# Eight of thirty bases of a graph layer summed by TensorE in column groups, and loads moved to another queue

## The chip, the cores and the metric

The kernel runs on one core of a Trainium2 chip, as one launch. The metric is the device time in microseconds of that launch; the profile describes one execution of it, and its span goes from the first to the last instruction of the trace.

## The reference

The input is a graph of N = 625 nodes with H = 512 features and E = 10000 edges of two relations. All is float32. Three blocks are computed:

```python
xn = layernorm(x)
# graph block: two layers; row, col = src, dst
w = einsum('rb,bio->rio', att, basis)        # 30 bases of 512x512 -> 2 relation matrices
msg_r = sigmoid(xn[col] @ gate_w[r])[:, None] * xn[col] @ w[r]     # by the edge's relation
h = relu(segment_sum(msg, row) + xn @ root1 + bias1)
out = the same with h, basis2, att2, gate_w2, root2, bias2
# mix block: linear attention with random features over xn, then a dense pair
x = x + out + mix(xn)
# feed-forward block: a shared expert, and two banks of 8 experts with top-1 routing
x = x + ffn(layernorm(x))
```

What matters here is `w`: for each layer, 30 bases of 1 MB are read from memory and summed into two matrices (r = 0, 1), each base with a coefficient `att[r, b]`.

## The kernel before

There is a fast path (`tile_fast`) and a general one, which runs only if a flag says that the edges are not sorted as expected; in these runs the fast path gives the result. All lines below are of the fast path.

The nodes stand in NT = 5 tiles of 125 (TP); the features in KC = 4 blocks of 128. A matrix of 512x512 is held as 128 partitions x 4 x 512.

**The stream of bases.** `relation_weights(l)` (L798) builds `wrel[l]`, 128 x 2 x 4 x 512, for layer l. For each of the 30 bases it issues a load of 1 MB on SP's queue (L806) into one of three slots of the tile `bases`, and then two operations, one per relation: the first base is scaled by ScalarE (L811), each later base is multiplied by its coefficient and added by VectorE (L813, scalar_tensor_tensor over 2048 elements in each of 128 partitions). A slot is loaded again when its two operations are done. Both layers' streams are written out early, with a low priority (`tc.cur_priority` raised by 100000): a scheduler at build time puts each instruction into its engine's program by priority and by the times that it expects, and on the chip each engine then goes through its own program in that order.

**The order on each engine.** On VectorE, operations of the stream stand between the operations of the rest of the kernel. On TensorE the order is: the mix block, with the counting of edges between it (L932, one-hot matrices that give `cnt`, how many edges lead from node to node by relation); then layer 1, `gathered` (L1026) and `through` (L1049); then layer 2 in the same way; then the feed-forward block.

`gathered(l, src, gate)` multiplies the features by the gates, as a high part (ScalarE, L1035) and a low rest (VectorE, L1036), and sums over the edges by matmuls with `cnt` (L1044), evacuated by ScalarE (L712). `through(t, ...)` makes one node tile of a layer's output in one PSUM tile by `narrow` (L762, matmuls at L765): a bias row, four matmuls with `root`, eight with `wrel[l]`. Layer 1's output goes through a relu on ScalarE to `gpre` (L1057). Layer 2 needs `gpre` transposed (`flip`, L743; matmuls at L748), its gates (`gates`, L771; ScalarE's exponential at L780, VectorE at L781 and L782), then `gathered`, then `through` (L1139), after which VectorE adds and normalizes.

**Buffers.** Tiles with a tag share memory in turn. In SBUF: "w8" has three buffers, through which wk, wv, wq, wo, w1, w2, root1, root2 and ws go; "A" to "D", "X" and "U" have one each; `yp`, opened after the mix block, has four buffers "y". In PSUM there are `pp` (two tiles of 1024 columns), `pc` (one such tile, tag "cnt") and `pn` (two tiles of 512). After the mix block `wide_ps` (L736) takes every third tile from `pc`.

**Loads other than bases.** They are issued by POOL's queue: wo, w1, w2, the roots (L663), x a second time (`again`, L1060, into the buffer "A" that `xnT` leaves), the shared expert's weights `ws` (L1073), the first weights of both banks (`load_first`, L1093), the second ones of the second bank (L1101). The second weights of the first bank are on SP (L1101, into the buffer that `bases` leaves).

Of the kernel before, what the change touches and what calls it, by code (L numbers as in the profile page):

```python
# [18 lines left out]
N = 625  # L19
H = 512  # L20
# [17 lines left out]
BASES = 3  # L38
MARGIN = 2
STEPS = [range(max(0, EC // NT * m - MARGIN), min(EC, EC // NT * (m + 1) + MARGIN)) for m in range(NT)]  # L40
WIN = 128
NW = (N + NX * (WIN - 1)) // WIN
WHOLE = 1.5 * 2 ** 23
# [544 lines left out]
def tile_fast(ctx: ExitStack, tc: tile.TileContext, a: dict, out: bass.AP, flag):  # L588
# [173 lines left out]
    def narrow(pairs, m=TP, n=H):  # L762
        ps = pn.tile([128, 512], F32, tag="narrow", name="ps_narrow")
        for i, (s, mv) in enumerate(pairs):
            nc.tensor.matmul(ps[:m, :n], s, mv, start=(i == 0), stop=(i == len(pairs) - 1))  # L765
        return ps[:m, :n]

    def nodes(t):
        return slice(t * TP, (t + 1) * TP)
# [14 lines left out]
    def columns(rows, name):  # L784
# [9 lines left out]
    between = {1: lambda: load_w(wkqv[:, 2 * H:3 * H], "wv", nc.sync),  # L794
               2: lambda: load_w(wkqv[:, H:2 * H], "wq", nc.sync)}
    came = {}

    def relation_weights(l):  # L798
        basis = a["L0_gnn_basis1" if l == 0 else "L0_gnn_basis2"]
        w = main.tile([128, 2, KC, H], F32, name=f"wrel{l}")  # L800
        wrel[l] = w
        here = tc.cur_priority
        tc.cur_priority = here + 100000
        for b in range(NB):
            src = bases[:, (l * NB + b) % BASES, :]
            nc.sync.dma_start(src.rearrange("p (k f) -> p k f", k=KC), basis[b].rearrange("(k p) f -> p k f", p=128))  # L806
            for r in range(2):
                dst = w[:, r].rearrange("p k f -> p (k f)")
                s = att_b[l][:, r * NB + b:r * NB + b + 1]
                if b == 0:  # L810
                    nc.scalar.activation(dst, src, AF.Copy, scale=s)  # L811
                else:
                    nc.vector.scalar_tensor_tensor(dst, src, s, dst, op0=ALU.mult, op1=ALU.add)  # L813
            if l == 0 and b in between:
                came[b] = between[b]()
        tc.cur_priority = here

# [21 lines left out]

    relation_weights(0)
    relation_weights(1)
    wv, wq = came[1], came[2]


# [179 lines left out]
    def gathered(l, src, gate):  # L1026
        aggT = main.tile([128, 2, KC, NP], F32, tag="U", name=f"agg{l}")
        for r in range(2):
            for half in range(2):
                hs = slice(half * HF, (half + 1) * HF)  # L1030
                high = yp.tile([TP, NT, HF], F32, tag="y", name=f"high{l}", bufs=4)
                low = yp.tile([TP, NT, HF], F32, tag="y", name=f"low{l}", bufs=4)
                for t in range(NT):
                    s = gate[:, t, r:r + 1]
                    nc.scalar.activation(high[:, t, :].bitcast(F32R), src[:, t, hs], AF.Copy, scale=s)  # L1035
                    nc.vector.scalar_tensor_tensor(low[:, t, :].bitcast(F32R), src[:, t, hs], s, high[:, t, :],  # L1036
                                                   op0=ALU.mult, op1=ALU.subtract)
                for k in range(KC // 2):
                    ks = slice(k * 128, (k + 1) * 128)
                    ps = wide_ps("ps_agg").rearrange("p (s n) -> p s n", s=2)  # L1040
                    pairs = [(y[:, m, ks].bitcast(F32R), m) for y in (high, low) for m in range(NT)]
                    for i, (y, m) in enumerate(pairs):
                        for s in range(2):
                            nc.tensor.matmul(ps[:, s, :SEG], y, cnt[:, r, m, s * SEG:(s + 1) * SEG].bitcast(F32R),  # L1044
                                             start=(i == 0), stop=(i == len(pairs) - 1))
                    evac(aggT[:, r, half * 2 + k, :].rearrange("p (s n) -> p s n", s=2), ps[:, :, :SEG])
        return aggT

    def through(t, srcT, root, aggT, w, more):  # L1049
        return narrow([more] + [(srcT[:, k, nodes(t)], root[:, k, :]) for k in range(KC)]  # L1050
                      + [(aggT[:, r, k, nodes(t)], w[:, r, k, :]) for r in range(2) for k in range(KC)])

    agg1 = gathered(0, xn, gate1)
    gpre = fourth("C", "gpre")
    for t in range(NT):
        ps = through(t, xnT, root1, agg1, wrel[0], (all_rows, brow[:, 1, :]))
        nc.scalar.activation(gpre[:, t, :], ps, AF.Relu)  # L1057

    again = fourth("A", "x_again", (TP + 2, NT, H))
    load_rows(again, a["x"], nc.gpsimd)  # L1060
    for i, nm in enumerate(("L0_mix_b2", "L0_gnn_bias2")):
        s = a[nm]
        nc.gpsimd.dma_start(again[TP + i:TP + i + 1], bass.AP(tensor=s.tensor, offset=s.offset,
                                                             ap=[[0, 1], [0, NT], [1, H]]))
    gT = fourth("B", "gT", TALL)
    flip(gT, gpre)
    gates(gate2, gT, col["gate2"], "ps_gate2")
# [1 line left out]

    ws = main.tile([128, 2, KC * FF], F32, tag="w8", name="ws", bufs=3)
    nc.gpsimd.dma_start(ws[:, 0, :].rearrange("p (k f) -> p k f", f=FF),  # L1073
                        a["L0_ffn_Ws1"].rearrange("(k p) f -> p k f", p=128))
    nc.gpsimd.dma_start(ws[:, 1, :], a["L0_ffn_Ws2"])
    ws1, ws2 = ws[:, 0, :].rearrange("p (k f) -> p k f", f=FF), ws[:, 1, :]

    wr = const.tile([128, KC, 2, NX], F32, name="wr")
    b2x = yp.tile([2 * NX + 1, H], F32, tag="y", name="b2x", bufs=4)
    br_b = const.tile([TP, 2, NX], F32, name="br_b")  # L1080
    for i, nm in enumerate(("sp", "fq")):
        s = a["L0_ffn_br_" + nm]
# [5 lines left out]
    def load_first(nm, tag, more):  # L1088

        t1 = main.tile([128, NX * KC * FF + more], F32, tag=tag, name="we1_" + nm)  # L1090
        s1 = a["L0_ffn_W1_" + nm]
        for e in range(0, NX, 2):
            nc.gpsimd.dma_start(t1[:, e * KC * FF:(e + 2) * KC * FF].rearrange("p (x f) -> p x f", f=FF),  # L1093
                                s1[e:e + 2].rearrange("e (k p) f -> p (e k) f", p=128))
        return t1

    def load_second(nm, tag, more, eng):

        t2 = main.tile([FF, NX * H + more], F32, tag=tag, name="we2_" + nm)
        for e in range(0, NX, 4):  # L1100
            eng.dma_start(t2[:, e * H:(e + 4) * H].rearrange("f (e d) -> f e d", d=H),  # L1101
                          a["L0_ffn_W2_" + nm][e:e + 4].rearrange("e f d -> f e d"))
        return t2

    we1 = [load_first("sp", "wrel0", 0), load_first("fq", "cnt", NW * WIN)]
    we2 = [load_second("sp", "basis", NW * WIN, nc.sync)]


    before = const.tile([TP, TP], F16, name="before")
    nc.gpsimd.memset(before, 1.0)  # L1110
    nc.gpsimd.affine_select(before, before, compare_op=ALU.is_ge, fill=0.0, base=-1, pattern=[[1, TP]],
                            channel_multiplier=-1)
    every = const.tile([TP, 128], F16, name="every")
    nc.gpsimd.memset(every, 1.0)
    lower = const.tile([2 * NX, 2, 2 * NX], F32, name="lower")
    nc.gpsimd.memset(lower, 1.0)
# [38 lines left out]


    G = 2 * NT
    work = yp.tile([128, 2 * NT * HF // 2], F32, tag="y", name="work", bufs=4)
    used = [0]

    def small_tile(*shape):

        n = 1
        for d in shape[1:]:
            n *= d
        used[0] += n
        names = "abcd"[:len(shape) - 1]
        return work[:shape[0], used[0] - n:used[0]].rearrange(
            f"p ({' '.join(names)}) -> p {' '.join(names)}", **dict(zip(names, shape[1:])))
# [221 lines left out]
```

## Time and profile before

| | us |
|---|---|
| median of 3 runs | 554.82 (553.94 to 555.72) |
| the profiled execution | 553.96, span 552.2 |
| PE (TensorE) busy | 454.8, 82% of the span |
| DVE (VectorE) busy | 394.8, 71% |
| of it the stream's 116 operations (L813) | 266.1, mean 2.346 |
| ACT (ScalarE) busy | 187.5, 34% |
| POOL busy | 58.4, 11% |
| chain that ended last | PE 68%, DVE 12%, issue 8%, DMA 7% |
| DMA | 98.29 MB, mean 178 GB/s |

PEld is the weight load of TensorE, which overlaps its matmuls. A float32 matmul appears in the records as two, each with its weight load. "Idle before" with a name after an arrow says how long an engine stood still before an instruction, and what ended the wait. A line number is that of the helper that issues the instruction, so the tiles' names tell groups of one line apart. Busy time is an average over stages: a change is judged by the stage in which it stands.

### The profile page before, as it was taken

What the parts mean: (1) busy time and instruction counts of PE and PEld (TensorE: products, weight loads), DVE (VectorE), ACT (ScalarE), POOL (GpSimd) and SP (SyncE); (2) the same over time, 40 slices, a digit from 0 to 9 for tenths busy, and PEclk for the clock granted to TensorE, in tenths of its full rate; (3) what the DMA queues carried; (4) which work ended last, traced back from release to release, by engine and by line L of the source; (5) the groups of instructions that cost most, each with busy time, mean ns of one, the idle gap of its engine ahead of it and who ended that gap; (6) DMA issues with size and microseconds to landing.
All of it is one profiled execution on the core that took longest, in us unless ns stands there. A gap on an engine that the chain in (4) does not pass through costs nothing.

```text
span 552.2 us, 5413 instructions
## 1 busy us (share of the span) xinstructions
PE 454.8 (82%) x1881; PEld 282.8 (51%) x1881; DVE 394.8 (71%) x477; ACT 187.5 (34%) x304; POOL 58.4 (11%) x105
## 2 busy tenths in 40 slices
PE   1799999999998999999997995009999999966800
PEld 0553486776567547934446992004446556556200
DVE  3789899989898999899997998993221445233311
ACT  2741299979776203500003630000001302321200
POOL 6400000000000000000012011000001080040040
PEclk9999999999897999999997899558999759987955
DMA  8967754633513485767679569634003251440532
GB/s 218 402 233 245 264 179 151 228 98 133 199 61 122 153 286 210 236 216 233 228 239 318 223 203 362 204 146 161 29 19 97 93 144 44 166 132 25 225 105 90
DMA packets 49171, 98.29 MB, mean 178 GB/s; under 512 B 5870, under 2 KB 5994, under 8 KB 49138
## 3 DMA queue, kind: packets, MB, share of 16 engines
q1 hardware_dynamic: 40322, 78.95, 42.0%
q0 software_dynamic: 8816, 18.93, 10.9%
q8 instruction: 17, 0.28, 0.2%
q14 instruction: 16, 0.13, 0.1%
HBM read 89.00 MB, written 8.85 MB: 177 GB/s over the span
## 4 chain that ended last, share of the span: by engine, by line
PE 68%; DVE 12%; issue 8%; DMA 7%; ACT 2%; POOL 1%; DVEq 0%; SPq 0%; POOLq 0%; ACTq 0%
PE ps_narrow L765 39%; PE ps_wide L759 10%; DVE wrel L813 7%; PE ps_agg L1044 5%; PE ps_hid L1329 4%; PE ps_cnt L932 3%; DMA got<-back,slot_i 3%; DMA basis_sb<-in_L_gnn_basis_dram 2%; PE ps_gate L777 2%; PE ps_flip L748 2%; DMA x<-in_x_dram 1%; POOL got L1339 1%; DVE oh_source L929 1%; PE ps_router L1175 1%; PE ps_sT L1320 1%
## 5 line engine op out<-in xcount | busy, mean ns | idle before, releaser
L813 DVE SCALAR_TENSOR_TENSOR wrel<-basis_sb,att,wrel 128x2048 f32<-128x2048 f32 x116 | 266.1, 2346 | 8.6 <-ACT wrel L811 4.4
L765 PE MATMUL ps_narrow<-wrel,agg 128*125 128x512 f32 x160 | 72.2, 606 | 34.2 <-DVE wrel L813 34.2
L927 ACT ACTIVATE side<-iota_h,ed_f 125x630 f16<-125x630 f16 x96 | 71.8, 812 | 7.0 <-PE ps_cnt L932 7.0
L765 PEld LDWEIGHTS ps_narrow<-wrel,agg 128*125 128x125 f32 x160 | 30.7, 193 | 74.3 <-issue 39.1
L932 PEld LDWEIGHTS <-oh_source 125*125 125x125 f16 x192 | 25.9, 139 | 27.2 <-issue 16.9
L932 PE MATMUL ps_cnt<-side,oh_source 125*125 125x315 f16 x192 | 39.0, 305 | 0.2
L1044 PE MATMUL ps_agg<-cnt,high 125*128 125x314 f32 x160 | 29.3, 332 | 5.8 <-ACT high L1035 3.5
L1044 PEld LDWEIGHTS ps_agg<-cnt,high 125*128 125x128 f32 x160 | 26.2, 206 | 6.4 <-ACT high L1035 3.5
L1140 DVE TENSOR_TENSOR v<-v,ps_narrow 125x512 f32<-125x512 f32 x5 | 3.4, 688 | 36.3 <-PE ps_narrow L765 36.3
L725 ACT ACTIVATE ln_rs<-ln_mv,eps 125x1 f32<-125x1 f32 (+1 forms) x7 | 2.1, 299 | 79.8 <-DVE ln_mv L1142 79.8
L929 DVE TENSOR_SCALAR oh_source<-iota_h,col_m,ed_f 125x128 f16<-125x128 f16 x96 | 25.0, 310 | 5.4 <-PE ps_cnt L932 5.4
L1044 PE MATMUL ps_agg<-cnt,low 125*128 125x314 f32 x160 | 27.7, 316 | 0.0
L1342 DVE SCALAR_TENSOR_TENSOR v<-got,work,v 125x512 f32<-125x512 f32 x10 | 7.5, 752 | 24.8 <-DMA got<-back,slot_i 24.8
L1044 PEld LDWEIGHTS ps_agg<-cnt,low 125*128 125x128 f32 x160 | 24.9, 194 | 0.2
L1335 DVE COPY stage<-ps_narrow 128x512 f32<-128x512 f32 x12 | 8.3, 691 | 21.9 <-PE ps_narrow L765 21.9
L1329 PE MATMUL ps_hid<-sort_fq,stage 128*128 x96 | 15.2, 335 | 8.7 <-DVE stage L1326 7.2
L1057 ACT ACTIVATE gpre<-ps_narrow 125x512 f32<-125x512 f32 x5 | 3.0, 597 | 54.6 <-PE ps_narrow L765 54.6
L759 PE MATMUL ps_wide<-zT,wq 128*128 128x512 f32 (+1 forms) x64 | 20.6, 433 | 0.0
L1329 PEld LDWEIGHTS ps_hid<-sort_fq,stage 128*128 128x128 f32 x96 | 14.8, 249 | 9.0 <-issue 7.3
L1339 POOL DMA_INDIRECT got<-back,slot_i x10 | 12.2, 1221 | 66.9 <-DVE sort_fq L1321 32.4
L765 PE MATMUL ps_narrow<-root,xnT 128*125 128x512 f32 x40 | 18.5, 605 | 0.0
L765 PE MATMUL ps_narrow<-wv,zT 128*125 128x512 f32 x40 | 18.4, 603 | 0.0
(271 smaller groups left out, 684.7 us busy)
## 6 DMA issues: line engine op xcount, KB each, us to landing
basis_sb<-in_L_gnn_basis_dram SPq DMA_DIRECT2D x60, 1024.0 KB
back<-stage SPq DMA_DIRECT2D x24, 256.0 KB
w<-in_L_mix_W_dram POOLq DMA_DIRECT2D x2, 1024.0 KB, 5.7
root<-in_L_gnn_root_dram POOLq DMA_DIRECT2D x2, 1024.0 KB
we_sp<-in_L_ffn_W_sp_dram POOLq DMA_DIRECT2D x4, 512.0 KB, 12.3
we_fq<-in_L_ffn_W_fq_dram POOLq DMA_DIRECT2D x4, 512.0 KB, 9.8
we_sp<-in_L_ffn_W_sp_dram SPq DMA_DIRECT2D x2, 1024.0 KB
we_fq<-in_L_ffn_W_fq_dram POOLq DMA_DIRECT2D x2, 1024.0 KB, 5.9
```

Source lines behind the costliest of these rows:

```text
L748: nc.tensor.transpose(ps[:, t, :TP], src[:, t, k * 128:(k + 1) * 128], ident[:TP, :TP])
L759: nc.tensor.matmul(ps[:, lo:hi], s, m[:, lo:hi], start=(i == 0), stop=(i == len(pairs) - 1))
L765: nc.tensor.matmul(ps[:m, :n], s, mv, start=(i == 0), stop=(i == len(pairs) - 1))
L777: nc.tensor.matmul(ps[:TP, 2 * t:2 * t + 2], srcT[:, k, nodes(t)], gw[:, k, :], start=(k == 0), stop=(k == KC - 1))
L813: nc.vector.scalar_tensor_tensor(dst, src, s, dst, op0=ALU.mult, op1=ALU.add)
L927: later(lambda: nc.scalar.activation(side, iota_h[:EP], AF.Sign, bias=row_f[:, c:c + 1]))
L929: later(lambda: nc.vector.tensor_scalar(os, iota_h[:EP, :128], col_m[:, m, c:c + 1], code_f[:, c:c + 1], op0=ALU.is_equal, op1=ALU.mult))
L932: nc.tensor.matmul(ps[:TP, s, :SEG + 1], os[:, :TP], side[:, s * SEG:(s + 1) * SEG + 1], start=(c == STEPS[m][0]), stop=(c == STEPS[m][-1]))
L1044: nc.tensor.matmul(ps[:, s, :SEG], y, cnt[:, r, m, s * SEG:(s + 1) * SEG].bitcast(F32R), start=(i == 0), stop=(i == len(pairs) - 1))
L1329: nc.tensor.matmul(ps, w1s[:, k * FF:(k + 1) * FF], sortT[i][:, k * N:][:, bass.ds(start[w], WIN)], start=(k == 0), stop=(k == KC - 1))
L1335: (nc.vector.tensor_copy if w % 2 else nc.scalar.copy)(y, ps)
L1339: nc.gpsimd.indirect_dma_start(yg[:, t, :], None, back_d[i][:, :], bass.IndirectOffsetOnAxis(ap=slot_i[:, 2 * t + i:2 * t + i + 1], axis=0))
```

## The change

Layer 2's stream is cut to 22 bases. The last eight (QUADS = 2 groups of four) are loaded by POOL into a tile of their own, `quad`, in a buffer of "w8". For each block k of 128 rows and each group q, four loads of 256 KB bring 128 rows of four bases, so that partition 32 j + p holds, for c = 0 to 3, row 32 c + p of base j. A stationary matrix `coef[:, q, r, :]` of 128 x 32 (four identity matrices of 32 x 32, each times its coefficient, made by 16 operations of POOL) then sums the four bases: a matmul for each r and c writes 32 rows, at partitions 32 c, of a PSUM tile of the tag "cnt". After both groups VectorE adds that tile to `wrel[1][:, :, k, :]`.

x is loaded again, and the two biases with it, through SP at priorities that follow the stream's (`stream[0]`), as are the first expert weights of both banks and the second ones of the first bank. In `through` the bias row comes after the root matmuls. `ws`, the routing masks `before` and `every`, and the biases with `mT` (`seconds`) lie in buffers "y" in place of tiles of their own.

```diff
+QUADS = 2
...
+    stream = [None]
     def relation_weights(l):
...
         here = tc.cur_priority
-        tc.cur_priority = here + 100000
-        for b in range(NB):
+        tc.cur_priority = stream[0] or here + 100000
+        for b in range(NB if l == 0 else NB - 4 * QUADS):
...
+        stream[0] = tc.cur_priority
         tc.cur_priority = here
+    def coefficients():
+        coef = const.tile([128, QUADS, 2, 32], F32, name="coef")
+        for q in range(QUADS):
+            for r in range(2):
+                for j in range(4):
+                    p = slice(32 * j, 32 * j + 32)
+                    c = r * NB + NB - 4 * (QUADS - q) + j
+                    nc.gpsimd.tensor_scalar(coef[p, q, r, :], ident[p, 32 * j:32 * j + 32], att_b[1][p, c:c + 1],
+                                            None, op0=ALU.mult)
+        return coef
+
+    def quads(coef):
+        t_ = main.tile([128, KC, H], F32, tag="w8", name="quad", bufs=3)
+        for k in range(KC):
+            ps = pc.tile([128, 2, H], F32, tag="cnt", name="ps_quad")
+            for q in range(QUADS):
+                for j in range(4):
+                    b = NB - 4 * (QUADS - q) + j
+                    nc.gpsimd.dma_start(t_[32 * j:32 * j + 32], a["L0_gnn_basis2"][b, k * 128:(k + 1) * 128, :]
+                                        .rearrange("(c p) f -> p c f", p=32))
+                here = tc.cur_priority
+                tc.cur_priority = here - 3000
+                for r in range(2):
+                    for c in range(4):
+                        nc.tensor.matmul(ps[32 * c:32 * c + 32, r, :], coef[:, q, r, :], t_[:, c, :],
+                                         start=(q == 0), stop=(q == QUADS - 1))
+                tc.cur_priority = here
+            nc.vector.tensor_tensor(wrel[1][:, :, k, :], wrel[1][:, :, k, :], ps, op=ALU.add)
...
     relation_weights(0)
     relation_weights(1)
+    coef = coefficients()
...
     def through(t, srcT, root, aggT, w, more):
-        return narrow([more] + [(srcT[:, k, nodes(t)], root[:, k, :]) for k in range(KC)]
+        return narrow([(srcT[:, k, nodes(t)], root[:, k, :]) for k in range(KC)] + [more]
                       + [(aggT[:, r, k, nodes(t)], w[:, r, k, :]) for r in range(2) for k in range(KC)])
 
     agg1 = gathered(0, xn, gate1)
+    quads(coef)
...
     again = fourth("A", "x_again", (TP + 2, NT, H))
-    load_rows(again, a["x"], nc.gpsimd)
+    here = tc.cur_priority
+    tc.cur_priority = stream[0]
+    load_rows(again, a["x"])
...
-        nc.gpsimd.dma_start(again[TP + i:TP + i + 1], bass.AP(tensor=s.tensor, offset=s.offset,
+        nc.sync.dma_start(again[TP + i:TP + i + 1], bass.AP(tensor=s.tensor, offset=s.offset,
...
+    stream[0] = tc.cur_priority
+    tc.cur_priority = here
...
-    ws = main.tile([128, 2, KC * FF], F32, tag="w8", name="ws", bufs=3)
+    ws = yp.tile([128, 2, KC * FF], F32, tag="y", name="ws", bufs=4)
...
-    b2x = yp.tile([2 * NX + 1, H], F32, tag="y", name="b2x", bufs=4)
+    seconds = yp.tile([2 * NX + 1, H + N], F32, tag="y", name="seconds", bufs=4)
+    b2x = seconds[:, :H]
...
-            nc.gpsimd.dma_start(t1[:, e * KC * FF:(e + 2) * KC * FF].rearrange("p (x f) -> p x f", f=FF),
-                                s1[e:e + 2].rearrange("e (k p) f -> p (e k) f", p=128))
+            nc.sync.dma_start(t1[:, e * KC * FF:(e + 2) * KC * FF].rearrange("p (x f) -> p x f", f=FF),
+                              s1[e:e + 2].rearrange("e (k p) f -> p (e k) f", p=128))
...
+    here = tc.cur_priority
+    tc.cur_priority = stream[0]
     we1 = [load_first("sp", "wrel0", 0), load_first("fq", "cnt", NW * WIN)]
     we2 = [load_second("sp", "basis", NW * WIN, nc.sync)]
-    before = const.tile([TP, TP], F16, name="before")
+    tc.cur_priority = here
...
+    before = small_half(TP, TP)
...
-    every = const.tile([TP, 128], F16, name="every")
+    every = small_half(TP, 128)
...
-    mT = yp.tile([2 * NX + 1, N], F32, tag="y", name="mT", bufs=4)
+    mT = seconds[:, H:]
```

More of the change, by code (lines that the diff above doesn't have):

```diff
@@ L1103, in load_second, with small_tile, small_half @@
         return t2
+    here = tc.cur_priority
+    tc.cur_priority = stream[0]
     we1 = [load_first("sp", "wrel0", 0), load_first("fq", "cnt", NW * WIN)]
     we2 = [load_second("sp", "basis", NW * WIN, nc.sync)]
-    before = const.tile([TP, TP], F16, name="before")
+    tc.cur_priority = here
+    work = yp.tile([128, 2 * NT * HF // 2], F32, tag="y", name="work", bufs=4)
+    used = [0]
+    def small_tile(*shape):
+        n = 1
+        for d in shape[1:]:
+            n *= d
+        used[0] += n
+        names = "abcd"[:len(shape) - 1]
+        return work[:shape[0], used[0] - n:used[0]].rearrange(
+            f"p ({' '.join(names)}) -> p {' '.join(names)}", **dict(zip(names, shape[1:])))
+    def small_half(p, n):
+        used[0] += (n + 1) // 2
+        return work[:p, used[0] - (n + 1) // 2:used[0]].bitcast(F16)[:, :n]
+    before = small_half(TP, TP)
     nc.gpsimd.memset(before, 1.0)
@@ L1157, in tile_fast @@
     G = 2 * NT
[L1158 to L1169, printed above, removed]
     lg = small_tile(TP, G, NX)
```

## The prediction

> **What bounds the kernel now.** I read the waits first, then the order in time of VectorE and of TensorE around the longest wait on the chain that ended last, then windows. In the list of waits (engine and line, what it waited for, total, times, longest) the largest on TensorE is one wait for the second layer's weights:
>
> ```profile
> PE ps_narrow L765 <- DVE wrel L813: 34.2, 1, 34.2
> ```
>
> VectorE in order of time (start, length, line, tiles, count, idle before):
>
> ```profile
> 234.98 63.44 DVE L813 SCALAR_TENSOR_TENSOR wrel<-basis_sb,att,wrel 128x2048 f32<-128x2048 f32 x28 [2.45 <-DMA basis_sb<-in_L_gnn_basis_dram]
> 301.32 0.17 DVE L781 TENSOR_SCALAR gate<-gate 125x10 f32<-125x10 f32 x1 [2.89 <-ACT gate L780]
> ...
> 343.13 31.77 DVE L813 SCALAR_TENSOR_TENSOR wrel<-basis_sb,att,wrel 128x2048 f32<-128x2048 f32 x14 [1.75 <-DMA basis_sb<-in_L_gnn_basis_dram]
> ```
>
> Before 298.4 VectorE has done 30 of layer 2's 58 steps (2.27 us each: 63.44/28). It then breaks off for gate2 and the low halves, so that TensorE can aggregate in the meantime; the last step ends at 372.6. TensorE in order of time:
>
> ```profile
> 304.53 2.98 PE L1044 MATMUL ps_agg<-cnt,high 125*128 125x314 f32 x10 [3.46 <-ACT high L1035]
> ...
> 334.92 3.60 PE L765 MATMUL ps_narrow<-root,gT 128*125 128x512 f32 x8
> 372.69 15.94 PE L765 MATMUL ps_narrow<-wrel,agg 128*125 128x512 f32 x32 [34.16 <-DVE wrel L813]
> ```
>
> Aggregation and the root terms of two node tiles are done by 338.5; only the weights are missing. Windows (window, length, busy and count by engine, TensorE clock, DMA share, GB/s):
>
> ```profile
> 234.60:292.20 57.60, 57.60 (x131) 23.63 (x132) 57.22 (x26) 3.07 (x5) 2.47 (x4) 1.00 0.72 231
> 304.50:329.80 25.30, 25.27 (x161) 25.27 (x162) 25.16 (x28) 12.38 (x26) 1.56 (x3) 0.92 0.57 199
> 372.70:376.00 3.30, 3.30 (x4) 1.48 (x5) 2.19 (x1) 0.00 (x0) 0.00 (x0) 0.50 0.03 2
> 372.70:422.10 49.40, 49.40 (x112) 21.60 (x113) 11.29 (x21) 1.18 (x4) 0.21 (x1) 0.96 0.19 64
> ```
>
> So the aggregation of layer 2 costs 25.3 us, hidden behind VectorE today; and after a pause TensorE runs at clock 0.50 for 3.3 us, 0.85 us per record against 0.43 later (6.87 us for 16).
>
> **The skill.** "TensorE: Matmul & The Clock Gate", section "Measured speedup vs the span model", gives 2.38x for three column tiles; no trace here shows column groups. The same page, "Loop structure matters more than you think", says that a DMA wait between bursts of matmuls leaves TensorE cold; the window at clock 0.50 agrees. "VectorE: DVE Perf Modes", "Why PSUM operands drop a tier": an fp32 operation with a PSUM operand runs at 1x; the row of L1140 agrees (688 ns for 512 elements). "DMA: Bandwidth & Descriptors", "Anatomy of one DMA", fits a transfer at 2.0 us plus bytes/436e3, an estimate of 2.6 us for 256 KB; here small loads from POOL took 4.0 to 5.5 us, so I use the trace.
>
> **The change part by part.** Removed: 8 bases x 2 = 16 VectorE steps, 16 x 2.27 = 36.3 us, so 42 steps are left. Added there: four additions of 128x1024 out of PSUM, 2 x 0.69 = 1.4 us each. Net, 30.7 us of VectorE.
>
> What decides is the order. In the changed program as built, VectorE has all 42 steps, then the four additions, and only then gate2 and the low halves. TensorE has the first two groups of eight quad matmuls inside layer 1's output, and the other six (48 matmuls) in one piece ahead of the last transposes of gpre, the gates, and all of layer 2's aggregation. The PSUM tile of a quad is the tag "cnt", with one buffer: k=1 cannot begin until k=0's addition is done, which stands behind the 42 steps. The buffer in SBUF is also one: each of the eight 1 MB fills (four DMAs from POOL) waits for the matmuls that read the fill before. Behind the blocked quads on TensorE stand the last transpose, gates, and so ScalarE's high halves, VectorE's low halves and the aggregation. The cover that aggregation had is gone.
>
> *Steps end.* 30 steps at 298.4 as now, then 12 x 2.27 = 27.2, without the 2.9 us wait for the gate. x_again now stands on SP's queue after layer 2's 16th basis and waits until TensorE has read xnT: 234.6 + 4 x 11.54 + 3.5 = 284.3, plus two quad groups of 3.9 = 292. The 17th basis, needed at 298.4, is behind its 1.12 MB; 2.1 MB at some 317 GB/s (231 GB/s at share 0.72) are 6.7, plus 2 us: 300.9, a stall of 2.5. The first addition ends at 298.4 + 27.2 + 2.5 + 1.4 = 329.5.
>
> *One group of eight matmuls.* Each fp32 matmul is two records on one column group, so I let only the second record of one overlap the first of the next: 9 slots for 16 records. Warm 9 x 0.43 = 3.9; cold, four slots at 0.85 and five at 0.43 = 5.6. Bounds: full overlap, four slots cold, 3.4; none, 16 slots, 8.6.
>
> *One fill.* Four issues on POOL of 0.52 to 0.55 us (rows of L1085), the last 1.65 after the first, and landing:
>
> ```profile
> we_fq<-in_L_ffn_W_fq_dram POOLq DMA_DIRECT2D x2, 1024.0 KB, 5.9
> ws<-in_L_ffn_Ws_dram POOLq DMA_DIRECT2D x2, 256.0 KB, 6.6
> ```
>
> 1.65 + 5.3 = 7.0; bounds 1.65 + 3.4 = 5 and 1.65 + 6.8 = 8.5.
>
> *The chain.* The first group of k=1 is loaded long before. Then five fills remain, each followed by its matmuls; the additions of k=1 and k=2 hide in fills. 5.6 + 5 x (7.0 + 5.6) + 1.4 = 70.0, so the last addition ends at 399.5.
>
> *After it.* Transposes 1.0 (cold), copy 0.6, gates 5.4, then gate to high half 3.5 as between 301.1 and 304.5: 10.5. Aggregation 25.3. Output: now only one tile has its root terms ready, so 8 x 0.87 = 7.0 and 4 x 11.16 (one tile, 399.63 to 410.79 now) = 51.6. It ends at 399.5 + 10.5 + 25.3 + 51.6 = 486.9, against 422.1: +64.8.
>
> *The start.* 16 small POOL operations for the coefficients wait for the second att load (issued 2.6, landing about 8.3) and stand ahead of the fills of "bad", two small loads and the rows2 loads. At about 0.2 us each (a 16x32 cast here took 0.20) POOL reaches rows2 at 13.6 rather than 12.83; columns2 at 21.1 waits for their landing. +1, bounds 0 and 4. VectorE's first read of "bad" at 14.5 is not reached.
>
> *At nothing.* Expert weights on SP behind the stream: first used some 40 us after layer 2's output ends, a cover of over 100 us; ws, second biases and the small masks in freed y buffers: filled during the 51.6 us of output, used after it; root terms ahead of the bias row: same work. The two early quad groups (7.8 us) delay TensorE where it later waits anyway. Without these covers, each load would cost its 6 to 12 us. The tail after 422.1 (130 us) only moves.
>
> Sum: +65.8. The profiled execution took 553.96 with span 552.2; the median, 554.82, is 0.9 above it. 554.8 + 65.8 = 620.6; I say 620.
>
> **The rivals.**
> 1. Column groups overlap in full: early groups 1.7, stall nothing, first addition 327.0; 3.4 + 5 x 10.4 + 1.4 = 56.8; +50 with the start, 605. For it, the skill's 2.38x; against, two records per matmul on one group.
> 2. No overlap: early groups 7 each put x_again to 298.3 and stall the stream 8.7; first addition 335.7, then 8.6 + 5 x 15.6 + 1.4 = 88: +90, 645.
> 3. Faster: the additions run as soon as TensorE has summed a quad, not after the 42 steps. Then the six groups go behind layer 1's output without VectorE, and VectorE, with gate and low halves between, ends at 298.4 + 2.9 + 27.2 + 5.6 + 8.2 = 342.3 rather than 372.6: 525. It decides where the last addition ends before 399.5 - 64.8 = 334.7. The order as built speaks against it: five fills cannot fit into the 5 us after the first addition.
>
> **How the numbers follow.** Chances: 0.51 for 620 (its own range, from fills of 5 to 8.5 us, 610 to 629), 0.22 each for rivals 1 and 2, 0.03 for rival 3, 0.02 for something between it and no change. The range takes in rivals 1 and 2 with the shorter and longer fills: 594 to 652. A change within 0.3% is about what a measurement of this kernel cannot tell from none. Slower 0.95, same 0.01, faster 0.04.
>
> **What would show it.** Right: TensorE idle with waits for VectorE from about 300 to 329, then for DMAs of the quad tile five times at some 12 us spacing; VectorE idle 60 us after its 42nd step; layer 2's aggregation after 400, not at 304; an output of 51 us after it. Groups of eight in 3.4, 5.6 or 8.6 us tell the cases apart. Wrong: the additions standing between steps, or the aggregation running before 335.

## The result, and the profile after

| | before | after |
|---|---|---|
| median, us | 554.38 (552.82 to 555.72, 4 runs) | 619.35 (617.79 to 621.47, 4 runs) |
| ratio, with its 95% interval | | 1.1139 (1.1092 to 1.1186) |
| span of the profiled execution | 552.2 | 619.8 |
| layer 1's output begins | 234.5 | 246.4 |
| layer 2's aggregation begins | 304.5 | 414.1 |
| layer 2's output ends | 422.1 | 489.3 |

The kernel is 11.4% slower. The span is 67.6 longer, and 67.2 of that has come together by the end of layer 2's output. The trace is that of the slowest of the four runs (621.47); between the medians the difference is 65.0. The list of waits of the changed kernel (engine and line, what it waited for, total, times, longest) has lost TensorE's single wait of 34.2 for `wrel`. In its place stand:

```profile
ACT gT L713 <- PE ps_flip L749: 91.4, 3, 90.7
DVE wrel L850 <- PE ps_quad L847: 58.5, 3, 21.1
PE ps_quad L847 <- DMA quad<-in_L_gnn_basis_dram: 39.0, 5, 9.0
PE ps_quad L847 <- DVE wrel L850: 26.3, 1, 26.3
```

From the bottom up, these are the order of events. TensorE waits once for VectorE's first addition, then five times for a fill of the quad tile; VectorE waits three times for the sums of a block; and ScalarE's copy of the last transposes, from which gates and aggregation of layer 2 follow, waits behind all of it. VectorE in order of time (start, length, line, tiles, count, idle before):

```profile
247.25 90.59 DVE L815 SCALAR_TENSOR_TENSOR wrel<-basis_sb,att,wrel 128x2048 f32<-128x2048 f32 x40 [2.43 <-DMA basis_sb<-in_L_gnn_basis_dram]
337.95 1.22 DVE L850 TENSOR_TENSOR wrel<-wrel,ps_quad 128x1024 f32<-128x1024 f32 x1
355.58 1.22 DVE L850 TENSOR_TENSOR wrel<-wrel,ps_quad 128x1024 f32<-128x1024 f32 x1 [16.41 <-PE ps_quad L847]
377.89 1.22 DVE L850 TENSOR_TENSOR wrel<-wrel,ps_quad 128x1024 f32<-128x1024 f32 x1 [21.09 <-PE ps_quad L847]
400.08 1.22 DVE L850 TENSOR_TENSOR wrel<-wrel,ps_quad 128x1024 f32<-128x1024 f32 x1 [20.97 <-PE ps_quad L847]
410.58 0.17 DVE L782 TENSOR_SCALAR gate<-gate 125x10 f32<-125x10 f32 x1 [9.28 <-ACT gate L781]
```

Forty steps run without a break, where before VectorE left the stream at 298.4 for the gate. Only then come the additions, and only after the fourth does the gate. TensorE in order of time:

```profile
247.36 1.92 PE L847 MATMUL ps_quad<-quad,coef 128*32 128x512 f32 x16
...
339.22 3.64 PE L847 MATMUL ps_quad<-quad,coef 128*32 128x512 f32 x16 [26.34 <-DVE wrel L850]
351.88 3.64 PE L847 MATMUL ps_quad<-quad,coef 128*32 128x512 f32 x16 [9.02 <-DMA quad<-in_L_gnn_basis_dram]
...
396.48 3.54 PE L847 MATMUL ps_quad<-quad,coef 128*32 128x512 f32 x16 [7.36 <-DMA quad<-in_L_gnn_basis_dram]
401.36 0.75 PE L749 MATMUL ps_flip<-ident,gpre 125*128 125x125 f32 x5 [1.34 <-DVE wrel L850]
402.88 7.45 PE L778 MATMUL ps_gate<-colv,gT 128*125 128x2 f32 x36 [0.77 <-ACT gT L713]
```

A group of eight matmuls (16 records) takes 1.92 in the early output of layer 1 and 3.64 after a wait. The windows of the chain, of the aggregation and of the output (window, length, busy and count of PE, PEld, DVE, ACT and POOL, TensorE's clock, DMA share, GB/s):

```profile
338.00:401.30 63.30, 21.75 (x96) 4.00 (x96) 4.83 (x4) 0.00 (x0) 10.93 (x20) 0.57 0.46 116
414.00:438.00 24.00, 24.00 (x163) 23.72 (x162) 6.44 (x16) 9.99 (x21) 3.47 (x8) 1.00 0.09 25
437.80:489.30 51.50, 51.50 (x122) 22.48 (x121) 9.10 (x20) 3.14 (x6) 0.20 (x1) 1.00 0.20 61
```

In the first, TensorE works a third of the time at clock 0.57 and VectorE 4.8 of 63.3. The second is the aggregation, which the stream of bases covered before and which now stands open on the path.

### The profile page after: what moved, and what is told of

The parts are those of the page before. It is cut to its first block, busy times and chain, and to the rows that moved or that the text cites. A ratio compares the mean times of both kernels' runs of the same rounds, so it can differ in the third digit from the quotient of the medians.

```text
span 619.8 us, 5708 instructions
## 1 busy us (share of the span) xinstructions
PE 484.4 (78%) x2009; PEld 291.3 (47%) x2009; DVE 363.5 (59%) x465; ACT 187.7 (30%) x304; POOL 72.4 (12%) x141
## 5 line engine op out<-in xcount | busy, mean ns | idle before, releaser
L815 DVE SCALAR_TENSOR_TENSOR wrel<-basis_sb,att,wrel 128x2048 f32<-128x2048 f32 x100 | 229.5, 2345 | 6.9 <-ACT wrel L813 4.4
L847 PE MATMUL ps_quad<-quad,coef 128*32 128x512 f32 x128 | 25.6, 941 | 65.4 <-DMA quad<-in_L_gnn_basis_dram 39.0
L766 PE MATMUL ps_narrow<-wrel,agg 128*125 128x512 f32 x160 | 70.8, 595 | 0.0
L847 PEld LDWEIGHTS ps_quad<-quad,coef 128*32 128x32 f32 x128 | 4.8, 146 | 85.0 <-issue 57.1
L850 DVE TENSOR_TENSOR wrel<-wrel,ps_quad 128x1024 f32<-128x1024 f32 x4 | 4.9, 1221 | 58.6 <-PE ps_quad L847 58.5
L841 POOL DMA_DIRECT2D quad<-in_L_gnn_basis_dram x32 | 17.5, 554 | 164.3 <-PE ps_quad L847 147.9
L713 ACT COPY gT<-ps_flip 128x625 f32<-128x625 f32 x4 | 2.6, 683 | 91.4 <-PE ps_flip L749 91.4
L1201 DVE TENSOR_TENSOR v<-v,ps_narrow 125x512 f32<-125x512 f32 x5 | 3.4, 688 | 45.7 <-PE ps_narrow L766 45.7
```

The source lines that it names most:

```text
L841: nc.gpsimd.dma_start(t_[32 * j:32 * j + 32], a["L0_gnn_basis2"][b, k * 128:(k + 1) * 128, :] .rearrange("(c p) f -> p c f", p=32))
L847: nc.tensor.matmul(ps[32 * c:32 * c + 32, r, :], coef[:, q, r, :], t_[:, c, :], start=(q == 0), stop=(q == QUADS - 1))
```

## The experiments

My theory: the order costs the time. The sums stand behind the whole stream of bases, each round of them waits for a fill of the one quad tile, and gates and aggregation stand behind the sums. Its rivals were that TensorE's sums are dear in themselves, that the other moved loads have a share, and, for the start, that something other than the coefficients delays it. Each ratio below is against runs of the kernel before on the same chip.

### The price of a group: does the order of the matmuls, or their place, make them overlap?

```diff
-                for r in range(2):
-                    for c in range(4):
+                for c in range(4):
+                    for r in range(2):
```

> The two inner loops of the quad sum are exchanged, so that the two matmuls of one column group follow each other instead of four different groups. Theory A (the eight matmuls of a group overlap because neighbours in the queue stand in different column groups): a group goes from 1.9 warm and 3.6 cold to 3 to 7, its five groups in the chain cost 4 to 17 more, 623 to 637. Theory B (order makes no difference, TensorE looks further ahead or the time is the stream of the rows and not of the group): 617 to 622 with unchanged groups.

Measured: 617.94 in one run. TensorE in order of time in this kernel:

```profile
244.06 1.94 PE L847 MATMUL ps_quad<-quad,coef 128*32 128x512 f32 x16
...
348.97 3.66 PE L847 MATMUL ps_quad<-quad,coef 128*32 128x512 f32 x16 [9.06 <-DMA quad<-in_L_gnn_basis_dram]
```

The groups take as long as before the exchange, 1.94 in layer 1's output and 3.66 in the chain. Theory B: whether neighbours in the queue share a column group makes no difference at this level. That does not yet say that the groups are the reason for the overlap, so in the next run all eight matmuls write one group:

```diff
-                        nc.tensor.matmul(ps[32 * c:32 * c + 32, r, :], coef[:, q, r, :], t_[:, c, :],
-                                         start=(q == 0), stop=(q == QUADS - 1))
+                        nc.tensor.matmul(ps[:32, r, :], coef[:, q, r, :], t_[:, c, :],
+                                         start=(q == c == 0), stop=(q == QUADS - 1 and c == 3))
...
-            nc.vector.tensor_tensor(wrel[1][:, :, k, :], wrel[1][:, :, k, :], ps, op=ALU.add)
+            nc.vector.tensor_tensor(wrel[1][:32, :, k, :], wrel[1][:32, :, k, :], ps[:32], op=ALU.add)
```

> All eight matmuls of a sum write the first column group (32 partitions), and the addition takes these 32 partitions alone, so that part of the computation is changed; fills, order and number of matmuls are those of the changed kernel. Theory A (the eight matmuls overlap because they stand in different column groups): without overlap a matmul of 512 columns takes its two records one after the other, 8 x 0.87 = 7 warm and 12 to 14 cold for a group instead of 1.9 and 3.6, and the chain's five groups add 25 to 50: 645 to 670. Theory B (they overlap for another reason): groups of 2 to 4, 614 to 622.

Measured: 659.05 in one run. TensorE in order of time in this kernel:

```profile
248.18 7.05 PE L847 MATMUL ps_quad<-quad,coef 128*32 128x512 f32 x16
...
374.75 9.75 PE L847 MATMUL ps_quad<-quad,coef 128*32 128x512 f32 x16 [7.47 <-DMA quad<-in_L_gnn_basis_dram]
```

Theory A holds: 7.05 instead of 1.92, so four groups in parallel are worth a factor of 3.67. The 7.05 is what 16 records take in layer 1's output too (7.13), so the sums lose their overlap and nothing more. The column group and the 32 partitions of PSUM that it writes change together here; the run doesn't separate them. "TensorE: Matmul & The Clock Gate" of the Trainium skill, section "Measured speedup vs the span model", gives 2.38 for three column tiles; this is the figure for four, with float32's two records per matmul. After a wait a group took 9.75 and not the 12 to 14 that I had expected: 2.70 over 7.05. At 7.05/16 = 0.44 a record and 0.88 at half speed, some 6 of the 16 records were slow, and full speed was back after 6.1 x 0.88 = 5.4, an estimate. Windows of 1 us in this group agree: the granted clock is 0.50 up to 380.0, which is 5.3 after the start, and 1.00 from 381.0.

### The fills

Only the first fill is left; the other seven groups multiply its data.

```diff
-                for j in range(4):
+                for j in range(4 if k == q == 0 else 0):
                     b = NB - 4 * (QUADS - q) + j
                     nc.gpsimd.dma_start(t_[32 * j:32 * j + 32], ...
```

> Only the first of the eight fills of the quad tile is loaded, the seven others are left out (so the other seven groups multiply the first group's bases: that part of the computation is changed); matmuls, additions and order are those of the changed kernel. Theory A (each round between additions is a fill of 7.8 and a group of 3.6, and the fills are what the chain waits for): the rounds shrink from 11 to 12.7 per group to about 3.7, the last addition comes near 339 + 5.3 x 3.7 + 4 additions = 362 to 368 instead of 400, and the time is 580 to 586. Theory B (the groups or the PSUM tile's reuse set the chain): it stays above 600.

Measured: 572.25 in one run, below Theory A's range. TensorE in order of time in this kernel:

```profile
337.38 5.07 PE L847 MATMUL ps_quad<-quad,coef 128*32 128x512 f32 x32 [26.76 <-DVE wrel L850]
343.80 3.64 PE L847 MATMUL ps_quad<-quad,coef 128*32 128x512 f32 x32 [1.35 <-DVE wrel L850]
348.78 3.64 PE L847 MATMUL ps_quad<-quad,coef 128*32 128x512 f32 x32 [1.34 <-DVE wrel L850]
```

The last addition ends at 353.7 instead of 401.3, 47.6 earlier, of which 1.9 are there at the first addition already; the time falls by 47.1. From the first addition to the last it is 45.7 less, while the waits for fills made up 39.0. So a fill cost more than its own wait: without it two groups (32 records) take 3.64, as one group does after a wait for a fill. The wait also leaves TensorE slow, as the same page of the Trainium skill says under "Loop structure matters more than you think": a DMA wait between bursts of matmuls makes the next one run cold. I had counted the wait and not the matmuls' speed, hence the 8 and more by which I missed.

### The other edits, without the sums

No base goes to TensorE and VectorE sums thirty again; the rest of the change stays. The second of the two runs also gives the moved loads back to POOL.

```diff
-QUADS = 2
+QUADS = 0
...
-    coef = coefficients()
...
-    quads(coef)
```

> No base goes to TensorE: coefficients, quad loads, quad matmuls and the four additions are left out and VectorE sums all thirty bases of layer 2 again; the changed order of x's second load and of the expert weights (behind the stream of bases on SP) stays. Theory A (the whole loss belongs to the quad sums): within 4 of the kernel before, 551 to 559. Theory B (the moved loads have a share of their own in the loss): 560 or more, with a wait on x_again or the expert weights in the chain.

> No base on TensorE, as in the run without sums, and x's second load and the expert weights issued on GpSimd as in the kernel before; what stays of the change is the order of the matmuls inside an output tile (root first, then the row of bias, instead of the row first). Theory A (the 3.1 that the run without sums lost came from the loads behind the stream): within 1.5 of the kernel before. Theory B (it came from the order of the matmuls or from how the start falls): 2 to 4 above it, with layer 1's output again 1 to 1.5 late.

Measured: 557.46 against 554.41, ratio 1.0059 (1.0036 to 1.0082), and with the loads on POOL 557.90 against 556.28, 1.0048 (1.0023 to 1.0073). The first is Theory A's by its number; the second, 1.6 above the kernel before, lies between its two theories. The sums thus carry nearly all of the loss. The other edits cost about half a per cent, and the queue of the loads isn't the reason, since giving it back changes nothing that can be told apart. The output of layer 1 begins 1.3 later than before in the first run's trace, at 235.8, and 4.6 later in the second's, at 239.1; the next part says where these differ. Which of the remaining edits costs the half per cent (root terms ahead of the bias row, or small tiles in "y") I didn't try.

### The start

First attempt: the call that makes the coefficients moves from the start to just ahead of `gathered(0, ...)`.

```diff
     relation_weights(1)
-    coef = coefficients()
...
+    coef = coefficients()
     agg1 = gathered(0, xn, gate1)
     quads(coef)
```

> The sixteen coefficient multiplications on GpSimd and the wait ahead of them are moved from the start to the end of GpSimd's layer 1 work, just ahead of the quad sums; all else is as in the changed kernel. Theory A (these instructions delay the rows2 loads of x and 'bad', and so z and the first column matmuls; the half clock that lasts longer follows from it): layer 1's output starts near 235 instead of 246.4, and the time falls from 619 by 10 to 13, to 606 to 609. Theory B (the coefficients cost the start about 1, as predicted, and the other 11 come from the other moved loads or from the clock): 616 to 620, and layer 1's output still starts past 243.

Measured: 617.33 against 554.41, ratio 1.1126 (1.1056 to 1.1196). By the number Theory B, but the edit didn't do what it says. POOL in order of time in this kernel:

```profile
10.10 8.93 POOL L830 TENSOR_SCALAR coef<-ident,att 32x32 f32<-32x32 f32 x16 [3.93 <-DMA att<-in_L_gnn_att_dram]
```

That is POOL, still busy with the coefficients from 10.1; this is TensorE, at the matmuls that make columns of rows2:

```profile
29.91 0.62 PE L766 MATMUL ps_narrow<-ident,rows 45*128 45x45 f32 x2 [8.46 <-DMA wr<-in_L_ffn_Wr_fq_dram]
```

The scheduler put the sixteen operations back into the first gap of POOL, ahead of its loads; only the memsets of `bad` came before them. One thing can be read from it: z was no longer late (17.5 instead of 20.4), the column matmuls still were, and the time hardly moved. So the wait for `bad` did not set the start. In the second attempt the tile of the coefficients takes the buffer "rows", which holds rows2 until TensorE has read it:

```diff
-        coef = const.tile([128, QUADS, 2, 32], F32, name="coef")
+        coef = main.tile([128, QUADS, 2, 32], F32, tag="rows", name="coef")
```

> The coefficients again, this time truly behind the start: their tile takes the buffer of rows2, so GpSimd cannot write it before TensorE has read rows2 (in the run before this one they still stood ahead of GpSimd's ten loads of rows2, wr and br_b; only the memsets of 'bad' had come before them). Theory A (the coefficients delay those loads, and through them the second column matmuls, at 29.9 there instead of 21.1): the column matmuls start near 22, layer 1's output near 236 to 238 instead of 246 to 247, time 606 to 611. Theory B (the delay of the start has another cause): column matmuls past 27, or layer 1's output past 243, time 615 to 620.

Measured: 612.61 against 555.16, ratio 1.1072 (1.1014 to 1.1131). TensorE in order of time in this kernel:

```profile
21.77 0.62 PE L766 MATMUL ps_narrow<-ident,rows 45*128 45x45 f32 x2 [0.61 <-DMA rows<-in_L_ffn_bs_dram]
```

In the changed kernel it is:

```profile
29.09 0.62 PE L766 MATMUL ps_narrow<-ident,rows 45*128 45x45 f32 x2 [4.63 <-DMA br_b<-in_L_ffn_br_fq_dram]
```

Before, they start at 21.10. Of the 8.0 by which they were late, 7.3 are gone: Theory A, for this part. The time ends between the two theories, because layer 1's output begins at 239.2, still 4.7 late. The traces split that. The gates of layer 1 begin at 164.2 before, 165.5 to 165.7 in this run and the two without sums, and 172.9 after. From there to layer 1's output it takes 70.4 before and 70.3 in the first run without sums, 73.5 or 73.6 in the other three. Where it takes longer, the gate matmuls (L778; L777 before) have a median of 348 ns instead of 248. So 7.2 of the 11.9 are the coefficients, some 1.4 come with the other edits, and 3.1 with TensorE running slower in the gates.

The 3.1 aren't tied to the change. The kernel with the loops exchanged differs from the changed one in the order of the sums' matmuls alone, and these come later. The gate matmuls of the changed kernel and of that one (count, shortest, median and longest in ns, first and last start):

```profile
L778 PE MATMUL ps_gate<-colv,xnT x40: 170/348/351, 172.9 to 180.2; 128*125 128x2 f32 x40
L778 PE MATMUL ps_gate<-colv,xnT x40: 170/248/350, 172.8 to 177.7; 128*125 128x2 f32 x40
```

With the loops exchanged it is 70.3 from the gates to layer 1's output (172.8 to 243.1). So the same work takes either value from one execution to another. Of the twelve traces of this case six have a median of 248 and six of 348, and both values occur with the early start and with the late one. In both kernels the granted clock falls from 1.00 to 0.50 within these gates: in the first it is 0.73 on average from 173.8 to 175.3 and 0.50 after that, in the second 1.00 up to 176.7 and 0.65 from there to 177.9. What decides the moment is open. The 1.4 isn't firm either: in the spread kernels with the loads on SP, which come next and keep these other edits, the gates begin at 164.2 and 164.4.

### The order

The same eight bases go to TensorE, with the same fills, matmuls and additions. The stream of the other 22 is cut by the additions, and the groups are spread through layer 1's output:

```diff
+            relation_weights(1, cuts[k], cuts[k + 1])
...
-    relation_weights(1)
+    relation_weights(1, 0, 4)
...
-    agg1 = gathered(0, xn, gate1)
-    quads(coef)
+    agg1 = gathered(0, xn, gate1, {5: 0})
+    quad_sum(1, coef)
     gpre = fourth("C", "gpre")
     for t in range(NT):
...
+        quad_sum(2 + t, coef)
...
     gates(gate2, gT, col["gate2"], "ps_gate2")
+    quad_sum(7, coef)
```

The first line stands behind the addition of block k, with cuts at 4, 9, 14, 19 and 22 bases; `quad_sum(i)` is the i-th fill and its eight matmuls, and group 0 stands behind the sixth block of layer 1's aggregation. The coefficients lie in the buffer "rows", as above, and the matmuls of the sums no longer have a raised priority. While sums are open, other tiles of PSUM don't take their turn in "cnt" around layer 2's transposes and gates. The first run has x's second load and the expert weights on POOL, the second on SP.

> The same eight bases by TensorE, the same matmuls, fills and additions, in another order: the stream of layer 2's other 22 bases is cut in five by the four additions (after 4, 9, 14 and 19 bases), the eight groups are spread through layer 1's output and the gates that follow it, coefficients as in the run with rows2's buffer, and x's second load and the expert weights are issued on GpSimd as in the kernel before. Theory A (the loss comes from the order: four additions behind the whole stream, with flip, gates and aggregation of layer 2 behind them): VectorE's stream ends 16 steps of 2.27 earlier and 4 additions of 1.22 later than before, 31 less, unless the aggregation becomes the bound; 520 to 535. Theory B (sums on TensorE cost more than they save wherever they stand, by their fills, by the clock and by TensorE's time in layer 1's output): 550 or more.

> As the run before it, with x's second load and the expert weights issued on SP behind the stream of bases, as in the changed kernel. Theory A (that move is worth 3 against the kernel, as in the run without sums on TensorE, 557.5 against 554.4): 2 to 5 above the run with these loads on GpSimd. Theory B (the move matters only where the stream is the bound): within 1.5 of it.

Measured: 549.96, ratio 0.9897 (0.9868 to 0.9927), and 546.96, 0.9888 (0.9831 to 0.9945). Both are about one per cent faster than the kernel before, where the run of 612.61, with the same sums and the coefficients in the same buffer but the old order, is 10.7% slower. The queue of the loads makes no clear difference here either: the two ratios agree. The medians are 3.0 apart, the second run being the lower, which is against Theory A of that run and outside the 1.5 of its Theory B. But neither reached the 520 to 535 of the first run's Theory A, and 549.96 lies at the edge of its Theory B. VectorE in order of time, in the second:

```profile
248.08 1.22 DVE L856 TENSOR_TENSOR wrel<-wrel,ps_quad 128x1024 f32<-128x1024 f32 x1 [2.64 <-PE ps_quad L853]
...
282.88 1.22 DVE L856 TENSOR_TENSOR wrel<-wrel,ps_quad 128x1024 f32<-128x1024 f32 x1 [10.83 <-PE ps_quad L853]
...
322.80 1.22 DVE L856 TENSOR_TENSOR wrel<-wrel,ps_quad 128x1024 f32<-128x1024 f32 x1 [6.56 <-PE ps_quad L853]
...
351.42 1.22 DVE L856 TENSOR_TENSOR wrel<-wrel,ps_quad 128x1024 f32<-128x1024 f32 x1 [2.67 <-PE ps_quad L853]
```

And TensorE in order of time, in the same run:

```profile
347.72 3.64 PE L853 MATMUL ps_quad<-quad,coef 128*32 128x512 f32 x16 [11.81 <-DMA quad<-in_L_gnn_basis_dram]
352.70 2.98 PE L1083 MATMUL ps_agg<-cnt,high 125*128 125x314 f32 x10 [1.33 <-DVE wrel L856]
```

The additions stand too early in the stream, so VectorE waits at them, and the last group stands too close behind the one before it, so TensorE waits for its fill with the aggregation behind it. Both are moved:

```diff
-    cuts = (4, 9, 14, 19) + (NB - 4 * QUADS,)
+    cuts = (3, 10, 17, 22) + (NB - 4 * QUADS,)
...
-    quad_sum(7, coef)
-    turn[0] = 0
-    agg2 = gathered(1, gpre, gate2)
+    agg2 = gathered(1, gpre, gate2, {1: 7})
+    turn[0] = 0
```

Groups 0 and 1 are also asked for inside layer 1's aggregation, and the others one tile earlier; and while sums are open, layer 2's aggregation leaves "cnt" to them.

> The spread order again (loads of x and expert weights on SP), with three things moved: the additions stand after 3, 10, 17 and 22 bases instead of 4, 9, 14 and 19; the last group stands inside layer 2's aggregation instead of ahead of it; and while sums are open, layer 2's aggregation uses the two 'wide' tiles of PSUM alone, so that none of its blocks waits for an addition. Theory A (in the spread run VectorE waited 10.8, 6.6 and 2.7 for sums and TensorE 11.8 for the last fill, and these waits now set the end): VectorE's stream ends near 352 instead of 369.5, and the time is 531 to 540. Theory B (TensorE's own work is the bound by then, the waits only fill its slack): within 3 of the spread run's 547.

Measured: 538.07 against 556.28, ratio 0.9708 (0.966 to 0.9756): Theory A by its time. VectorE in order of time in this kernel:

```profile
249.37 1.22 DVE L856 TENSOR_TENSOR wrel<-wrel,ps_quad 128x1024 f32<-128x1024 f32 x1 [8.23 <-PE ps_quad L853]
...
283.81 1.22 DVE L856 TENSOR_TENSOR wrel<-wrel,ps_quad 128x1024 f32<-128x1024 f32 x1 [1.42 <-PE ps_quad L853]
...
361.17 1.22 DVE L856 TENSOR_TENSOR wrel<-wrel,ps_quad 128x1024 f32<-128x1024 f32 x1 [2.55 <-PE ps_quad L853]
```

And TensorE in order of time:

```profile
338.66 1.92 PE L853 MATMUL ps_quad<-quad,coef 128*32 128x512 f32 x16
...
356.41 2.07 PE L766 MATMUL ps_narrow<-wrel,agg 128*125 128x512 f32 x2 [7.60 <-DVE wrel L816]
```

The wait at the second addition has shrunk from 10.83 to 1.42 and the one at the third is gone; at the first, which now stands a base earlier, it has grown from 2.64 to 8.23. Together they are 12.2 instead of 22.7. VectorE's last step ends at 358.6, not near 352. TensorE's wait for a fill is gone. It goes on with `wrel` at 356.4, where the kernel before did at 372.7, and the last addition ends at 362.4, where the stream before ended at 374.9. Seven of the eight groups take 1.92 or 1.93, because TensorE no longer waits ahead of them; the last runs only at 358.4, behind the aggregation and the wait of 7.60, and takes 2.68. The three moves were made together, so what each gave isn't shown. The wait of 7.60 for VectorE is left, so the bound is where it was in the kernel before, only earlier.

## Why the prediction was right, and where not

620 was predicted and 619.35 measured. The mechanism was right, and so were most sizes, but two terms were off in opposite directions, and that 620 came out is luck in part. Each is taken against the trace of the changed kernel.

- **The order.** As said: 42 steps, four additions, then gates, aggregation, output. TensorE waits for VectorE once and for DMAs five times; VectorE stands idle for 58.5 at the additions. That this order costs the time, and not the sums as such, is shown by the spread orders: 549.96, 546.96 and 538.07, against 612.61 in the old order.
- **Steps end and first addition.** With the +1 of the start, 330.5 was predicted for the end of the first addition; it came at 339.2. That is 8.7 later: layer 1's output came 10.9 later than predicted, and 2.2 of it were made up for. The steps began 12.3 later than before (247.25 against 234.98), 0.4 more than that output. The stall of 2.5 for x_again did not happen (no wait inside the forty steps): as the two early groups took 1.92 each and not 3.9, x_again was issued at 300.1, 8 later than I had it, while the steps, late with the start, came to the 17th basis some 12 later (247.25 + 28 x 2.265 = 310.7). The addition took 1.22, not 1.4.
- **One group.** This step failed: "I let only the second record of one overlap the first of the next: 9 slots". The four column groups run side by side nearly in full, 1.92 warm where I had 3.9 (7.05 / 4 = 1.76 would be in full). Rival 1 had the term nearly right (1.7 early, 3.4 in the chain; measured 1.92 and 3.64). Rival 2's price for no overlap, 7 warm, is what the run with one column group shows, 7.05; its 8.6 cold is 9.75.
- **One fill.** 7.0 was predicted; TensorE's five waits were 9.0, 7.7, 7.4, 7.6 and 7.4, mean 7.8. In the last, the fourth load is issued 1.6 after the first and landed 5.3 later (391.06 to 396.34), so these two terms were right. Left out were 0.3 from the matmuls' end to the first issue (389.11 to 389.43) and 0.1 from the landing to the next matmul. The first and longest wait has two loads of expert weights beside it: they are 2.10 of the 3.15 MB that moved from 338 to 351, where the window of the second fill has its own 1.05 MB alone. The 2.6 quoted for a load of 256 KB, which the sum didn't use, was too little here: the 32 loads landed a median of 4.9 after issue. And the "4.0 to 5.5 us" for small loads left out one of 10 KB that took 9.4.
- **The chain.** From the end of the first addition to the end of the last: 70.0 predicted, 62.1 measured. The groups made it 5 x 2.0 + 2.0 = 12 shorter, the fills 5 x 0.8 = 4 longer.
- **After it.** 87.4 predicted, 88.0 measured (401.3 to 489.3): gates of 7.45 for 36 records rather than 5.4 made the stretch ahead of the aggregation 12.8 instead of 10.5; the aggregation took 24 instead of 25.3; the output 51.5 against 51.6.
- **The start.** This term was mis-sized: +1 within bounds of 0 and 4, measured +11.9. Two of its sizes failed. A coefficient took 0.45 (7.27 for 16), not the 0.2 of a 16x32 cast; and the loads of rows2, wr and br_b stand in one queue behind them, so that their issues began at 17.8 (at 6.1 in the second run with late coefficients). I also wrote that VectorE's first read of `bad` "is not reached". It was, for 3.17, though the run that lifted that wait alone gained almost nothing. The runs give the coefficients 7.2 of the 11.9 and, less firmly, the other edits 1.4; the remaining 3.1 are the slower gates of this execution, which aren't tied to the change.
- **At nothing.** The expert weights and x behind the stream cost nothing that can be told from noise in the two pairs with and without that move, both of them kernels without the chain. In the chain two of these loads stand beside the first fill, whose wait of 9.0 is 1.4 to 1.7 longer than the others; how much of that is theirs no run separates. The tail moved only: 130.5 against 130.1.
- **Sum.** In the trace, 11.9 (start) - 2.2 (no stall, shorter addition) + 62.1 - 70.0 + 0.6 (after it) + 64.8 (the prediction without the start) + 0.4 (tail) = 67.6. The start's 10.9 too little was paid by a chain and a stall that were 10.1 too long. That is luck: with the start as measured, the prediction's own sum comes to 620.6 + 10.9 = 631.5, outside its range of 610 to 629, and Rival 1's to 605 + 10.9 = 616. The case of the groups that the runs bear out is the one of Rival 1, which had a chance of 0.22, and not the one that had 0.51.

**Rival 3** is what the run of 538.07 made of the kernel: additions between the steps. It was priced at 525 for an order that ends VectorE at 342.3; the best order tried ended it at 362.4. One reading was off by a step: "the last step ends at 372.6" is the end of relation 0's last step, on which TensorE goes on; the very last ends at 374.9 (343.13 + 31.77).

## What to carry to other kernels

Before work is moved from a busy engine to an idle one, look at what the result of the moved work waits for and at what stands behind it in each engine's program: an addition into a tile that a long stream also updates can't run until the stream does, unless the stream is cut there. The moved work's price then depends on its place, since the same eight groups cost 62 us on the path in one order and let the kernel gain 2.9% in another. A single buffer that is filled again between short bursts costs twice, by the wait and by the slow matmuls after it.

## What was not expected of the hardware

- Eight float32 matmuls of 512 columns in four column groups take 1.92, in one group 7.05; it made no difference (1.94) whether matmuls of one group followed each other directly.
- After a wait of 7.4 to 9 TensorE ran a whole group at half speed (3.64 instead of 1.92), and the longer groups of the run with one column group show it coming back after about 5.4. I had taken 3.3 from a window of the kernel before that ended too soon: the clock there is 0.50 up to 376 and 0.68 from 376 to 377, which puts its return some 3.9 after the start.
- A product of a 32x32 block with a scalar on POOL took 0.45 to 0.60 in three traces (7.27 for 16, 8.93 for 16, 7.83 for 13), more than twice the 16x32 cast that I had priced it by.
- The forty gate matmuls of layer 1 had a median of 248 ns in six traces and 348 ns in six, and a pair of kernels with the same program up to there has one of each. In that pair the granted clock falls to 0.50 sooner or later within these gates (after 175.3 it is 0.50 in one, up to 176.7 it is 1.00 in the other), and the time from the gates to layer 1's output is 73.5 or 70.3.
